# Copies and band writes issued by SyncE, and a new order of units and weights in the last part

## The chip, the core and the metric

The kernel runs on one core of a Trainium2 chip. A core has five engines that work side by side and meet at semaphores: TensorE (PE, matmuls; its weight loads are listed as PEld), VectorE (DVE), ScalarE (ACT), GpSimd (POOL) and SyncE (SP, which here only issues DMAs). Each engine executes its instructions in the order of the program. All DMAs, whoever issues them, are moved by the core's sixteen DMA engines. The metric is device time in microseconds; lower is better.

## The reference

All data is float32. The input x has the shape (2, 256, 64, 64). Two layers follow each other:

```python
# layer 0: full attention over the 4096 positions of an image, 8 heads of 32
q, k, v = conv1x1(x, Wq, bq) / sqrt(32), conv1x1(x, Wk, bk), conv1x1(x, Wv, bv)
fuse = softmax(q @ k.T) @ v
x = conv1x1(concat([x, fuse]), Wf, bf) * m + x * (1 - m)     # m: mask, resized bilinearly
# layer 1
x = x * sigmoid(relu(xp @ ca_w1 + ca_b1) @ ca_w2 + ca_b2)    # per position
x = x + window_attention(x)                                  # 8 x 8 windows, 4 heads of 64
x = channel_shuffle(x, groups=4)
y = relu(bn1(grouped_conv7x7(x, sa_w1)))                     # 64 groups: 4 channels in, 1 out
y = bn2(grouped_conv7x7(y, sa_w2))                           # 64 groups: 1 channel in, 4 out
return x * sigmoid(y)
```

What matters for the change is the pair of 7 x 7 convolutions at the end, and the attention loop ahead of it, since the preparation of the convolutions' weights runs beside that loop.

## The kernel before

**Three parts.** First come the projections: q, k and v of all sixteen chunks (two images of eight chunks, a chunk being 512 positions) are computed and written to DRAM. Then the attention loop runs over 1024 slots: for each image b, chunk c, half of the heads g and block m of 128 keys, PE computes four score matmuls (L632), ACT the exponentials (L642), PE the products with the values (L661), and DVE adds up the denominators (L663). Work on a finished chunk (fusion L731, layer 1's gate, the window attention up to L963) is cut into small stages which `run_stages` sets between the slots of the next chunk. The result of a chunk goes as rows to the DRAM tensor `x_s` (L978, `xs` in the profile). The last part is the pair of convolutions, as a generator `convolve` whose steps lie between the stages of the last chunk, and run alone after them.

**Order.** The program's order is written out by hand (`manual_schedule`): every engine executes what is emitted for it, in that order. SyncE's list in the loop is made of the key and value pieces (`load_piece`, L559 and L561, one piece for four slots, two pieces ahead, three buffers each), q, x and the mask of the next chunk. A load waits on SyncE until PE has left the buffer that it fills.

**Bands.** The convolutions are matmuls with banded weights. A unit is four groups of channels; there are NU = 16 units. The weights of unit u are one row block of the DRAM tensor `w_s` (`ws` in the profile): 128 x 1792 floats, 896 KB, of which most are zero. The generator `bands` fills it: sixteen copies of a block of zeros (L341), then 156 small DMAs from DRAM to DRAM which write the coefficients onto diagonals (L349, L355 and L362), in runs of 28 floats for the first convolution and of 7 floats for the second. `bands` is advanced by one DMA at every fifth slot (L1189). GpSimd issues all of them. Its other work in the loop is the storing of rows (L978). What is left of `bands` would be emitted at slot 960, before the generator `convolve` starts (L1171).

**Convolution items.** The list `items` (L987) holds pairs of a unit and the images that it is done for: units 0 to 6 for image 0 alone, which is complete before the last chunk is; units 2 to 6 for image 1; units 7 to 15 for both; and units 1 and 0 for image 1. `EARLY = 7` sets the border. For each item k the generator emits `conv1(k + 1)` (L1043 and L1051), `conv2(k)` (L1067, L1077, L1083) and `gate(k)` (L1089 and the stores of L1102). So on PE the first convolution of item k + 1 stands ahead of the second one of item k.

**Inputs of the items.** `load_x` (L1022) reads the rows: image 0's early items into four tiles `xe`, later ones into four tiles `xl`, which come free with the end of the loop. `more` issues the first four of these as soon as the last stage has been emitted, so on SyncE they stand there and wait for the rows of image 1 to land in `x_s`. `load_w` (L1015) reads a unit's weights: unit 0 into a tile of its own, all others into a ring of EB = 8 buffers that held the exponentials. Before the change, units 1 to 8 are loaded one behind the other when the loop ends, and units 9 to 15 and once more unit 1 (the list `again`) after an item that used a weight for the last time. Stores of `gate` alternate between GpSimd and SyncE; for early items that are stored after the last stage GpSimd issues all.

Of the kernel before, what the change touches and what calls it, by code (L numbers as in the profile page):

```python
# [17 lines left out]
B, C, H, W = 2, 256, 64, 64  # L18
# [11 lines left out]
AHEAD = 2  # L30
EB = 8
DN = 8
EARLY = 7
HEADS1, HD1 = 4, 64
WS = 8
NW = W // WS
# [10 lines left out]
NU = NG // UG  # L47
# [8 lines left out]
def conv_seq_kernel(ctx: ExitStack, tc: tile.TileContext, a, out):  # L56
    nc = tc.nc
# [68 lines left out]
    w_s = dram.tile([NU, P, 2 * 32 * UW], F32, name="ws")  # L126
# [33 lines left out]
    zero_s = dram.tile([P, 2 * 32 * UW], F32, name="zeros")  # L160
# [171 lines left out]
    def spread(row, n):  # L332
        f = row.shape[-1]
        return row.rearrange("p u f -> u p f").to_broadcast([NU, n, f])


    def bands():
        band1 = w_s.rearrange("u p (m f) -> u (p m) f", f=UW)
        band2 = w_s.rearrange("u p (m f) -> u (p m) f", f=UW // 4)
        for u in range(NU):  # L340
            nc.gpsimd.dma_start(w_s[u], zero_s)  # L341
            yield
        for q in range(4):
            for dy in range(KS):
                r0, r1 = max(0, dy - PAD), min(RB, RB + dy - PAD)
                p0, m0, n = 32 * q + 1 + r0, 1 + r0 - dy + PAD, r1 - r0
                k = KS * q + dy
                at0, step = p0 * 64 + m0, 64 + 1
                nc.gpsimd.dma_start(  # L349
                    band1[:, at0 : at0 + step * (n - 1) + 1 : step, :], spread(r1_s[k : k + 1], n)  # L350
                )
                yield
                for i in range(4):
                    at0, step = p0 * 256 + 128 + i * 32 + m0, 256 + 1
                    nc.gpsimd.dma_start(  # L355
                        band2[:, at0 : at0 + step * (n - 1) + 1 : step, :],
                        spread(r2_s[k : k + 1, :, i], n),
                    )
                    yield
            for i in range(4):  # L360
                at0 = 32 * q * 256 + 128 + i * 32 + 1
                nc.gpsimd.dma_start(  # L362
                    band2[:, at0 : at0 + RB, :], spread(r2_s[32 + q : 33 + q, :, i], RB)
                )
                yield
# [157 lines left out]
    def pipeline(arm, shifted, pools):  # L523
# [462 lines left out]

        items = [(u, (0,)) for u in range(EARLY)] + [(u, (1,)) for u in range(2, EARLY)]  # L987
        items += [(u, (0, 1)) for u in range(EARLY, NU)] + [(1, (1,)), (0, (1,))]
        staged = []

        def convolve():
# [8 lines left out]
                nc.gpsimd.memset(t, 0.0)  # L1000
                ycs.append(t)
            xs, ws, ys = {}, {}, {}
            again = deque([*range(1 + EB, NU), 1])
            dst = out.rearrange("b (g i) r w -> b i r g w", i=4)

            def load_w(u):
                if u >= NU:
                    return
                n = 2 * 32 * UW
                if u == 0:  # L1010
                    t = cpool.tile([P, n], F32, name=f"w{arm}{u}")
                else:
                    t = ep.tile([P, HG, CH], F32, tag="e", name=f"w{arm}{u}")
                    t = t.rearrange("p h n -> p (h n)")[:, 0:n]
                nc.sync.dma_start(t, w_s[u])  # L1015
                ws[u] = t

            def load_x(k):
                u, images = items[k]
                x = xs[k] = early[k % 4] if k < EARLY else xcs[k % 4]  # L1020
                for i, b in enumerate(images):
# [5 lines left out]
            def load_rows(k):  # L1027

                while len(xs) < min(k + 1, len(items)) and (
                    staged or B - 1 not in items[len(xs)][1]  # L1030
                ):
                    load_x(len(xs))

            def conv1(k):
                if k >= len(items):
                    return
                u, images = items[k]
                n = nb * len(images)
                w = ws[u][:, 0 : 32 * UW].rearrange("p (m g d) -> p g d m", g=UG, d=KS)
                s = psum1(f"c1{arm}{k}")  # L1040
                for d in range(KS):
                    for j in range(4):
                        nc.tensor.matmul(  # L1043
                            s[32 * j : 32 * j + 32, 0 : n * W],
                            w[:, j, d, :],
                            xs[k][:, 0:n, j, d : d + W],
                            start=(d == 0),
                            stop=(d == KS - 1),
                        )
                y = ys[k] = ycs[k % 2]  # L1050
                nc.scalar.activation(  # L1051
                    y[:, 0:n, PAD : PAD + W],
                    s[:, 0 : n * W].rearrange("p (n x) -> p n x", x=W),
                    AF.Relu,
                    bias=cbias1[:, u : u + 1],
                )

            def conv2(k):
                u, images = items[k]
                n = nb * len(images)  # L1060
                y = ys.pop(k)
                w = ws[u][:, 32 * UW :].rearrange("p (m d) -> p d m", d=KS)
                tiles = [psum2(f"c2{arm}{k}_{hh}") for hh in range(2)]
                for d in range(KS):
                    for j in range(4):
                        r = slice(32 * j, 32 * j + 32)
                        nc.tensor.matmul(  # L1067
                            tiles[j // 2][:, j % 2, 0 : n * W],
                            w[r, d],
                            y[r, 0:n, d : d + W],  # L1070
                            start=(d == 0),
                            stop=(d == KS - 1),
                        )
                z = pool.tile([P, 4, B * nb * W], F32, tag="z", name=f"z{arm}{k}", bufs=2)
                z = z[:, :, 0 : n * W]
                for hh in range(2):
                    nc.scalar.activation(  # L1077
                        z[:, 2 * hh : 2 * hh + 2, :],
                        tiles[hh][:, :, 0 : n * W],
                        AF.Tanh,  # L1080
                        scale=0.5,
                    )
                nc.scalar.activation(z, z, AF.Copy, bias=0.25, scale=0.25)  # L1083
                return z.rearrange("p j (n x) -> p j n x", x=W)

            def gate(k, z):
# [5 lines left out]
                if k == len(items) - 1:  # L1092
                    engines = (nc.scalar, nc.sync)
                elif staged and k < EARLY:
                    engines = (nc.gpsimd,)
# [12 lines left out]
            def more():  # L1108
                if staged and not xcs:

                    for n in range(3):
                        t = ep.tile([P, HG, CH], F32, tag="sum", name=f"xl{arm}{n}", bufs=3)
                        t = t.rearrange("p h n -> p (h n)")[:, 0 : B * nb * UG * WP]
                        xcs.append(t.rearrange("p (n g w) -> p n g w", n=B * nb, g=UG, w=WP))
                    xcs.append(pool.tile([P, B * nb, UG, WP], F32, name=f"xl{arm}3"))
                    load_rows(EARLY + 3)
                return bool(xcs)
# [2 lines left out]
            load_rows(3)  # L1120
            load_w(0)
            pool = yield
            for u in range(1, 1 + EB):
                load_w(u)
            conv1(0)
            yield
            for k, (u, images) in enumerate(items):
                while len(xs) <= k + 1 < len(items):
                    if not more():
                        yield  # L1130
                conv1(k + 1)
                yield
                more()
                z = conv2(k)
                yield
                more()
                gate(k, z)
                if xcs or k + 4 < EARLY:
                    load_rows(k + 4)

                if (u >= 2) == (B - 1 in images) and u and again:
                    load_w(again.popleft())

        def run_later():
            for _ in range(len(later)):
# [6 lines left out]
        def run_stages():  # L1152
            while stages:
# [3 lines left out]
                stages.popleft()  # L1157

        banded = bands()

        nc.scalar.activation(warm, ones[0:1, 0:1], AF.Exp)
# [132 lines left out]
```

## Time and profile before

| what | value |
|---|---|
| median of three runs | 3051.75 us (3051.0 to 3055.79) |
| the profiled execution | 3062.01 us, of it 3060.2 from first to last instruction |
| PE busy | 2967.3 us (97%) |
| DVE busy | 2498.5 us (82%) |
| ACT busy | 2478.7 us (81%) |
| POOL busy | 369.4 us (12%) |
| zero copies L341 | 16 of 896 KB, issued 188.8 to 216.1 us |
| band DMAs L349, L355, L362 | 156, issued 241.2 to 2346.2 us |
| weight loads L1015 | 17 of 896 KB, 2659.8 to 2980.1 us |
| attention loop | starts at 187.1 us |
| last part | about 2814 us to the end |

Busy time says how much of the span an engine had an instruction in work; the sum over parts with different limits hides where time is lost. Times in the views count from the first instruction. In a timeline, a line is start, length, engine, line of the code, operation, written tile, read tile, number of instructions, and in brackets how long the engine idled before and who released it. `SPq` stands for DMAs issued on SyncE's queue; `issue` stands for time in which the profile shows nothing that the engine waited for. Buffer numbers are left out of names, and an added `a` is the name of the arm of the program that is run (`ka` is a key piece).

### The profile page before, as it was taken

The page shows a single profiled execution, that of the slowest core. Times are in us where ns is not written, and L with a number is a line of the kernel's source. Part 1 is how long each engine was busy: PE and PEld are TensorE (multiplying, and loading weights), DVE is VectorE, ACT ScalarE, POOL GpSimd, SP SyncE. Part 2 cuts the span into 40 slices and gives each one's busy share as a digit, 9 for nine tenths or more (in the row PEclk, how much of TensorE's full clock was granted, in tenths as well). Part 3 has the DMA queues.
Part 4 walks back from the last instruction along what each step waited for, and adds up shares of the span by engine and source line. Part 5 has one row for each costly group of instructions (what it writes and reads, how often), then busy time and mean ns, then how long its engine had stood idle before and what let it go on. Part 6 is the DMA issues. An engine that isn't in the chain of part 4 may idle for free.

```text
span 3060.2 us, 60785 instructions
## 1 busy us (share of the span) xinstructions
PE 2967.3 (97%) x25114; PEld 1005.6 (33%) x25114; DVE 2498.5 (82%) x1347; ACT 2478.7 (81%) x4147; POOL 369.4 (12%) x636
## 2 busy tenths in 40 slices
PE   9968989999999999999999999999999999999897
PEld 3541222222322222232222232322222322223675
DVE  3227989899989999899999898999999898999211
ACT  5537969898989899898989898989898898988333
POOL 8020000101010101010100101010101000000256
PEclk9988999999999999999999999999999999999999
DMA  8574212424252424243322314242424232423364
GB/s 241 200 248 106 63 52 60 71 63 73 60 78 60 70 70 73 67 66 75 63 65 64 68 60 73 62 71 60 69 71 71 66 71 66 102 63 101 96 208 112
DMA packets 155999, 266.02 MB, mean 87 GB/s; under 512 B 43016, under 2 KB 61756, under 8 KB 155456
## 3 DMA queue, kind: packets, MB, share of 16 engines
q1 hardware_dynamic: 127424, 213.86, 25.3%
q0 software_dynamic: 23728, 45.48, 9.8%
q8 instruction: 200, 3.28, 0.5%
q10 hardware_dynamic: 4560, 2.70, 0.3%
q14 instruction: 87, 0.71, 0.1%
HBM read 213.49 MB, written 66.13 MB: 91 GB/s over the span
## 4 chain that ended last, share of the span: by engine, by line
PE 71%; DVE 13%; DMA 4%; issue 2%; ACT 2%; POOL 1%; SPq 0%; DVEq 0%; ACTq 0%
PE sa L632 29%; PE ava L661 27%; DVE suma L663 11%; PE qka L802 4%; PE hya L731 4%; DMA ka<-ks 2%; PE vwa L888 2%; ACT ea L642 1%; PE opa L952 1%; PE c2a L1067 1%; POOL out_dram L1102 1%; DMA wa<-ws 1%; PE c1a L1043 1%; PE sca L836 1%; PE rda L699 1%
## 5 line engine op out<-in xcount | busy, mean ns | idle before, releaser
L663 DVE TENSOR_TENSOR suma<-suma,ea 128x2048 f32<-128x2048 f32 x960 | 2198.7, 2290 | 122.7 <-ACT ea L642 39.5
L642 ACT ACTIVATE ea<-sa 128x512 f32<-128x512 f32 (+1 forms) x3072 | 2043.7, 745 | 122.0 <-PE sa L632 75.4
L632 PE MATMUL sa<-qa,ka 32*128 32x512 f32 x8192 | 1186.6, 641 | 39.7 <-DMA ka<-ks 38.2
L661 PE MATMUL ava<-ea,va 128*32 128x512 f32 x8192 | 1093.8, 605 | 0.3 <-ACT fa L671 0.3
L632 PEld LDWEIGHTS sa<-qa,ka 32*128 32x128 f32 x8192 | 331.2, 183 | 793.6 <-ACT ea L642 688.7
L661 PEld LDWEIGHTS ava<-ea,va 128*32 128x32 f32 x8192 | 161.8, 108 | 781.9 <-issue 755.7
L978 POOL DMA_DIRECT2D xs<-xo x94 | 66.1, 711 | 2302.4 <-DVE xo L963 2302.2
L1102 POOL DMA_DIRECT2D out_dram<-za x204 | 114.9, 571 | 102.4 <-DVE za L1089 55.5
L802 PE MATMUL qka<-ua,qkv_w 128*128 128x512 f32 x256 | 118.4, 605 | 0.0
L663 DVE TENSOR_TENSOR suma<-ea,ea 128x2048 f32<-128x2048 f32 x32 | 73.1, 2285 | 51.3 <-ACT ea L642 51.3
L1089 DVE TENSOR_TENSOR za<-za,xla 128x1536 f32<-128x1536 f32 (+1 forms) x16 | 22.6, 1409 | 110.0 <-ACT za L1083 56.7
L453 DVE TENSOR_REDUCE top<-sq 128x512 f32<-128x2048 f32 x16 | 36.6, 2286 | 81.4 <-ACT sq L447 81.4
L739 ACT ACTIVATE ta<-hya,bf 128x512 f32<-128x512 f32 x32 | 20.3, 684 | 99.7 <-PE hya L731 99.7
L1067 PE MATMUL c2a<-yca,wa 32*128 32x192 f32 (+1 forms) x1288 | 95.9, 440 | 4.0 <-issue 3.8
L1077 ACT ACTIVATE za<-c2a 128x384 f32<-128x384 f32 (+1 forms) x46 | 25.8, 615 | 86.3 <-DMA out_dram<-za 50.2
L743 DVE TENSOR_TENSOR ta<-ta,mca 128x512 f32<-128x512 f32 x32 | 22.0, 689 | 88.3 <-ACT ta L739 88.3
L1067 PEld LDWEIGHTS c2a<-yca,wa 32*128 32x128 f32 x1288 | 87.0, 314 | 14.9 <-issue 14.0
L857 ACT ACTIVATE ewa<-ewa,mxwa 128x64 f32<-128x64 f32 x256 | 85.5, 362 | 1.5 <-DVE mxwa L848 1.5
L355 POOL DMA_DIRECT2D ws<-r2s x112 | 69.7, 625 | 95.3 <-DMA ws<-r2s 48.6
L815 ACT ACTIVATE qka<-qka,qkv_b 128x512 f32<-128x512 f32 x64 | 40.7, 695 | 41.6 <-PE qka L802 41.6
L802 PEld LDWEIGHTS qka<-ua,qkv_w 128*128 128x128 f32 x256 | 46.0, 189 | 71.3 <-issue 58.7
L434 PE MATMUL q<-x,WqT 128*128 128x512 f32 x128 | 62.2, 631 | 5.6 <-DMA WqT<-in_WqT_dram 5.6
(141 smaller groups left out, 1620.5 us busy)
## 6 DMA issues: line engine op xcount, KB each, us to landing
ka<-ks SPq DMA_DIRECT2D x256, 256.0 KB
va<-vs SPq DMA_DIRECT2D x256, 256.0 KB
wa<-ws SPq DMA_DIRECT2D x17, 896.0 KB
ws<-zeros POOLq DMA_DIRECT2D x16, 896.0 KB, 23.9
xs<-xo POOLq DMA_DIRECT2D x78, 140.0 KB, 8.0
xla<-xs SPq DMA_DIRECT2D x25, 420.0 KB
x<-in_x_dram SPq DMA_DIRECT2D x16, 512.0 KB
qs<-qst SPq DMA_DIRECT2D x16, 512.0 KB
```

Of the source, the lines that this page charges most:

```text
L355: nc.gpsimd.dma_start(band2[:, at0 : at0 + step * (n - 1) + 1 : step, :], spread(r2_s[k : k + 1, :, i], n),)
L434: nc.tensor.matmul(s[:, g, :], w[:, kc, g * P : (g + 1) * P], rhs, start=(kc == 0), stop=(kc == KC - 1),)
L632: nc.tensor.matmul(heads[j], k[r, cols], q[r, g, :], start=True, stop=not shifted)
L642: nc.scalar.activation(e[:, h, :], tile, AF.Exp, scale=SCALE0)
L661: nc.tensor.matmul(av[r, :], v[:, m % PB, r], e[:, j, :], start=start, stop=stop)
L663: nc.vector.tensor_add(total, first[0] if m == 1 else total, e)
L731: nc.tensor.matmul(s[:, oc, :], wf[:, kc, oc * P : (oc + 1) * P], f[:, kc - KC, :] if half else xw[kc], start=(kc == 0), stop=(kc == 2 * K ...
L802: nc.tensor.matmul(s[:, j, :], wqkv[:, kc, o : o + P], u[:, kc, :], start=(kc == 0), stop=(kc == KC - 1),)
L857: nc.scalar.activation(e[:, n, :], e[:, n, :], AF.Exp, bias=mx[:, n : n + 1], accum_out=rs[:, n : n + 1],)
L978: eng.dma_start(x_s[b, n, p + r0 : p + r1].rearrange("r g w -> g r w"), xo[64 * h : 64 * h + 64, oc, r0 - WS * c : r1 - WS * c, :],)
L1067: nc.tensor.matmul(tiles[j // 2][:, j % 2, 0 : n * W], w[r, d], y[r, 0:n, d : d + W], start=(d == 0), stop=(d == KS - 1),)
L1102: engines[stores % len(engines)].dma_start(dst[b, i, r0:r1, UG * u : UG * u + UG, :], z[p + r0 : p + r1, :, nb * m + n, :],)
```

## The change

All DMAs of `bands`, the sixteen zero copies and the 156 band writes, are issued by SyncE in the place where GpSimd issued them. `EARLY` becomes 8: unit 7 is done for image 0 among the early items and for image 1 after them, and no longer for both at once. So there are 24 items and not 23. Of the weights, only units 1 and 2 are loaded when the loop ends; after the gate of each item one further unit is loaded, in the order 3 to 15 and then 1 again. After item 7 none is loaded.

```diff
-EARLY = 7
+EARLY = 8
@@ bands()
-            nc.gpsimd.dma_start(w_s[u], zero_s)
+            nc.sync.dma_start(w_s[u], zero_s)
...
-                nc.gpsimd.dma_start(
+                nc.sync.dma_start(
                     band1[:, at0 : at0 + step * (n - 1) + 1 : step, :], spread(r1_s[k : k + 1], n)
                 )
...
-                    nc.gpsimd.dma_start(
+                    nc.sync.dma_start(
                         band2[:, at0 : at0 + step * (n - 1) + 1 : step, :],
                         spread(r2_s[k : k + 1, :, i], n),
                     )
...
-                nc.gpsimd.dma_start(
+                nc.sync.dma_start(
                     band2[:, at0 : at0 + RB, :], spread(r2_s[32 + q : 33 + q, :, i], RB)
                 )
@@ convolve()
-            again = deque([*range(1 + EB, NU), 1])
+
+            weights = deque([*range(1, NU), 1])
...
-            for u in range(1, 1 + EB):
-                load_w(u)
+            for _ in range(2):
+                load_w(weights.popleft())
             conv1(0)
...
-                if (u >= 2) == (B - 1 in images) and u and again:
-                    load_w(again.popleft())
+                if weights and (k < EARLY - 1 or k >= EARLY):
+                    load_w(weights.popleft())
```

## The prediction

> **What bounds the kernel now.** I read the list of engines first (PE busy 97%, DVE 82%), then the waits, then PE's timeline round every wait over 1 us, then windows there. In the attention loop PE gives no time away: a chunk of 64 slots takes 163.2 us (the fusion matmuls of L731 start at 2206.14, 2369.32 and 2532.50 in the chain). So only two places can give time back, the start of the loop and the last part. PE's timeline at the start:
>
> ```profile
> 202.32 1.06 PE L661 MATMUL ava<-ea,va 128*32 128x512 f32 x8
> 241.08 2.09 PE L632 MATMUL sa<-qa,ka 32*128 32x512 f32 x8 [37.69 <-DMA ka<-ks]
> ```
>
> PE waits 37.69 us for the third key piece. SyncE issued that load at 192.12. Stretches of the same time (us, then busy time of PE, PEld, DVE, ACT, POOL, then clock, DMA share, GB/s), and the DMA view for the second stretch:
>
> ```profile
> 187.00:203.00 16.00, 15.61 (x112) 4.19 (x112) 10.13 (x5) 15.71 (x26) 6.47 (x13) 1.00 0.97 326
> 203.00:241.00 38.00, 0.39 (x4) 0.00 (x0) 5.91 (x3) 1.41 (x3) 2.44 (x5) 0.54 0.96 311
> ```
> ```profile
> q0 software_dynamic: 371, 10.21, 80.0%
> q1 hardware_dynamic: 863, 1.59, 15.6%
> ```
>
> All engines idle while the DMA engines run full: POOL's queue q0 holds 80% with the sixteen zero copies, SyncE's queue q1 gets 15.6% (packets, MB, share). Key pieces arrive when the zeros are through. DVE's timeline carries the loss on:
>
> ```profile
> 194.85 14.27 DVE L663 TENSOR_TENSOR suma<-suma,ea 128x2048 f32<-128x2048 f32 x6
> 245.19 2.29 DVE L663 TENSOR_TENSOR suma<-suma,ea 128x2048 f32<-128x2048 f32 x1 [36.07 <-ACT ea L642]
> 249.10 52.61 DVE L663 TENSOR_TENSOR suma<-suma,ea 128x2048 f32<-128x2048 f32 x22 [1.62 <-ACT ea L642]
> ```
>
> From 249.10 DVE runs without a gap until the first stage, and at 398.49 PE itself has waited 8.99 us and starts only when DVE's reciprocal (397.45) is there. So in the first chunk DVE sets the pace (2.39 us a slot against PE's 2.07), and what it lost, 36.07 + 1.62 = 37.69 us, is on the path. After 398 PE sets the pace.
>
> The last part, PE's timeline:
>
> ```profile
> 2833.75 2.65 PE L1067 MATMUL c2a<-yca,wa 32*128 32x192 f32 x40
> 2840.19 1.68 PE L1067 MATMUL c2a<-yca,wa 32*128 32x192 f32 x16 [3.79 <-issue]
> 2843.60 6.02 PE L731 MATMUL hya<-xa,WfT 128*128 128x512 f32 x8
> 2849.45 3.60 PE L731 MATMUL hya<-fa,WfT 128*128 128x512 f32 x8
> 2900.84 3.56 PE L1067 MATMUL c2a<-yca,wa 32*128 32x192 f32 x56
> 2908.44 4.72 PE L1043 MATMUL c1a<-xla,wa 128*32 128x192 f32 x56 [4.04 <-DMA xla<-xs]
> ```
>
> Two gaps: 3.79 us in the middle of a group of 56, with nothing waited for, and 4.04 us for the rows of image 1. The first lies inside the burst of eight weight loads. Stretches, and SyncE's queue:
>
> ```profile
> 2814.00:2842.00 28.00, 23.62 (x333) 13.75 (x334) 18.23 (x11) 12.92 (x22) 2.77 (x4) 0.93 0.93 283
> 2842.00:2853.00 11.00, 11.00 (x35) 5.25 (x31) 1.23 (x1) 2.58 (x5) 0.00 (x0) 0.71 0.01 5
> ```
> ```profile
> 2814.21 18.07 SPq L1015 DMA_DIRECT2D wa<-ws x8
> 2860.12 0.80 SPq L1022 DMA_DIRECT2D xea<-xs x1
> 2896.42 1.37 SPq L978 DMA_DIRECT2D xs<-xo x2
> 2904.72 1.99 SPq L1022 DMA_DIRECT2D xla<-xs x4
> ```
>
> The clock after the gap is 0.5 until about 2848.8: the same eight L731 matmuls take 6.02 us, then 3.60. From 2908.44 to 3043 PE has no gap over 0.2 us.
>
> **What the Trainium skill says.** "DMA: Bandwidth & Descriptors", section "Queues, rings and completion order": an engine takes turns between the queues at packet granularity. The trace agrees: in the stall q0's packets average 27.5 KB (10.21/371), q1's 1.8 KB (1.59/863), and q1 moves 1.59 MB in 38 us. The same page, "Issuing engines are not separate DMA queues": another issuer saves only issue time. That would leave the copies as heavy as before; here I count on their place in the order of issue, not on the issuer. "TensorE: Matmul & The Clock Gate", Part 1: after an idle window of about 3.4 us the clock halves. The trace agrees: 0.5 after 3.79 and after 4.04 us.
>
> **Part 1, zeros on SyncE.** POOL issues all sixteen at 188.84 to 216.09, held back by nothing but their own completions. SyncE executes in order between the key and value loads, which wait for PE (L559 and L561 waits). So it issues one per five slots: 5 x 2.07 = 10.3 us apart at least. One copy costs about 52/16 = 3.3 us of all DMA engines (188.8 to 241 for sixteen, other loads included). Piece 2 comes ahead of the first zero copy: 192.12 issue, 1.28 MB (x, mask, k, v) at 390 GB/s (loads reach 399 in the window at 2870) is 3.3 us, so by about 197, before the need at 203.4. Later pieces have 17.4 us between issue and first use (251.45 to slot 20, which is ten slots after the one at 248.13: 268.8) and are held 3.3 us at most. Gain 37.69. Bounds: 25 if later pieces stumble, 40 if more than DVE's own idle returns.
>
> **Part 2, bands on SyncE.** 156 DMAs (28 of L349, 112 of L355, 16 of L362); with the zeros 172 issues, which one per five slots ends at slot 860, before the flush at slot 960. POOL pays 0.62 us each; SyncE's small issues take 0.32 to 0.8 us, and it has waits of 4 to 5 us per load in which that disappears. Data: from 542 to 556 thirteen bands and two pieces keep the DMA share at 5.80 x 2 us = 11.6 us, so about 1 us a band. The trace shows no such band on q1. Lower bound 0.5; upper 14, the landing time with several in flight (medians of 9.3 to 13.9 for the forms of L355 and L362). I take 1 to 3 us. A piece has 17.4 us of cover, so nothing reaches PE: cost 0. POOL has nothing late behind it. No band waits long on SyncE: the first needs the sixteenth zero copy, issued about 10 us before; behind such a wait stand the key loads, again with 17.4 us.
>
> **Part 3, weights one at a time.** Only w1 and w2 are loaded at 2814. The burst (896 KB x 8) is gone, so I count the fetch gap and its slow clock away: L731's second half starts at 2842.1 instead of 2849.45 (c2 ends 2837.3, spreads 2838.4, 3.63 us for the first half; the other inputs, via ACT and DVE, are there by 2841). Gain 7.35; bounds 0 (the gap comes from something else) and 8.
>
> Against it, each weight now follows the gate three items earlier. A load issued at 2868.36 is in by about 2873.1 (windows: 399 and 220 GB/s, then 0), so 5 us. Relative to before: w3 goes out at 2861.0, in at 2866.5, wanted at 2866.09: 0.4. w5 out 2884.1, in 2889.5, wanted 2888.77: 0.7. w4 has 7 us to spare; w6 comes with what is lost already. Together 1.2.
>
> **Part 4, eight units early.** Unit 7 is done twice alone (2 x 5.98: 2.46 + 3.52) instead of once for both images (9.64): +2.32 us of PE. The extra early item should fill the 4.04 us gap, but its weights can't be there: w7 is issued after gate 4, and the four loads of image 1 rows stand ahead of it on SyncE, blocked until the stores have landed (2904.72, now 2906.5 with the 1.2 and w6 beside the stores). They took 7.1 us of traffic (to 2911.8), w7 another 2.4: in at 2916.5. On PE the first convolution of item 7 stands ahead of the second of item 6, so PE idles from 2905.6 to 2916.5. It resumes 2916.5 - 7.35 = 2909.15 against 2908.44: +0.7. Slow clock as before, +0.2.
>
> **Sum.** -37.7 (start) + 0.7 + 0.2 + 2.3 (last part, in which the 7.35 is used up) = -34.5. The profiled execution, 3062.01 (span 3060.2, 1.8 around it), becomes 3027.5. It lay 10.3 above the median of the runs, so I take the difference to the median: 3051.75 - 34.5 = 3017.
>
> **Rivals.**
> 1. Forecast, 3017, own range 3008 to 3027: chance 0.54.
> 2. The stall only shrinks: zero copies on the loads' own queue hold pieces 3 to 10 up. For: every load from 193 on now stands behind one. Against: 3.3 us against 17.4. About 17 us stay: 3034. 0.14 (0.01 of it within 0.2%).
> 3. The last part is better: w7 in time, 4.04 filled, no idle of 10.9: 3017 - 10 = 3007. The order on SyncE speaks against. 0.10.
> 4. The last part is worse: the gap in the group stays (+7.35) or weights come later: 3026. 0.09.
> 5. Slower: bands as small packets on q1 saturate the loads' queue. Five slots last 12.75 us (163.2/64 x 5) and carry 640 KB of loads, 1.65 us at 390 GB/s, so bands decide from about 11 us each; from 11.2 the 34.5 are lost (156 x 0.22), at 12, inside the upper bound, they cost 156 us: 3173. For: never seen on q1, runs of 28 bytes. Against: 1 us on q0. 0.13.
>
> **Numbers.** Three runs spread 3051.0 to 3055.79, so 0.2% (6 us) is what can be told. Faster 0.86, within 0.01, slower 0.13. Range 3004 to 3040: cases 1 to 4; case 5 stays out.
>
> **What would show it.** Right: no PE wait on ka<-ks over 1 us near 203, L341 on SPq about 10 us apart, the first c2a group whole near 2796 with clock 1.0, one PE gap of some 10 us ahead of a c1a, released by wa<-ws, then 24 items. Wrong: PE waits on ka or va spread over the loop every five slots (case 5), or a wait of tens of us near 200 (case 2); no gap at c1a (case 3).

## The result and the profile after

The changed kernel takes 3025.45 us (median of four runs, 3024.80 to 3025.97), the kernel before 3053.71 us in the same comparison (3051.00 to 3055.79). The ratio is 0.9908, with a 95% interval from 0.9891 to 0.9925: faster by 28.3 us. The forecast was 3017 us, 34.5 us faster. The profiled execution of the changed kernel took 3024.80 us (span 3023.0), 0.65 us below the median; that of the kernel before, 3062.01, had lain 8.3 us above the median.

Line numbers are one to two higher than before (L632 is L633, L1067 is L1069). In the names of tiles, `c1a` and `c2a` are the results of the first and second convolution, `hya` that of the fusion, `ca1a` that of layer 1's gate; items are counted from 0. First PE's timeline, the two longest waits between the start of the loop and the last part (the next ones are 1.10 us at 1668.48 and 1.09 us at 2647.93); a row is start, length, engine, line, operation, written and read tile, number of instructions, and the wait ahead of it:

```profile
187.35 3.06 PE L633 MATMUL sa<-qa,ka 32*128 32x512 f32 x16 [1.19 <-ACT vst L480]
361.21 1.01 PE L700 MATMUL rda<-inva,spread_h 32*128 32x128 f32 x6 [8.99 <-issue]
```

The 37.69 us wait for the third key piece is gone. The wait at the first stage, 8.99 us, is the same as before and 37.28 us earlier (398.49 to 361.21): PE still waits there for DVE. DVE's timeline shows why the whole gain came through, a run of additions without the hole of 36 us:

```profile
195.06 69.38 DVE L664 TENSOR_TENSOR suma<-suma,ea 128x2048 f32<-128x2048 f32 x29
```

SyncE's queue at the start shows the copies between the loads, and the same stretch of time as before shows what that does to all engines (us, busy time of PE, PEld, DVE, ACT, POOL, then clock, DMA share, GB/s):

```profile
193.25 0.42 SPq L562 DMA_DIRECT2D va<-vs  x1
193.73 0.59 SPq L342 DMA_DIRECT2D ws<-zeros  x1
194.45 0.48 SPq L560 DMA_DIRECT2D ka<-ks  x1
199.53 0.32 SPq L562 DMA_DIRECT2D va<-vs  x1
199.90 0.48 SPq L342 DMA_DIRECT2D ws<-zeros  x1
```
```profile
203.00:241.00 38.00, 38.00 (x300) 8.73 (x296) 36.34 (x17) 36.82 (x56) 0.00 (x0) 1.00 0.43 146
```

PE was busy for 0.39 us of these 38 and is now for all of them. The DMA engines are busy for 43% and not for 96%: the same sixteen copies are spread out to 368 us.

The last part on PE:

```profile
2792.98 3.58 PE L1069 MATMUL c2a<-yca,wa 32*128 32x192 f32 x56
...
2797.78 3.70 PE L732 MATMUL hya<-xa,WfT 128*128 128x512 f32 x8
2801.32 3.60 PE L732 MATMUL hya<-fa,WfT 128*128 128x512 f32 x8
...
2818.67 2.54 PE L1045 MATMUL c1a<-xea,wa 128*32 128x192 f32 x56 [0.65 <-DMA wa<-ws]
...
2843.36 2.55 PE L1045 MATMUL c1a<-xea,wa 128*32 128x192 f32 x56 [1.92 <-DMA wa<-ws]
...
2853.35 2.54 PE L1045 MATMUL c1a<-xea,wa 128*32 128x192 f32 x56 [0.32 <-DMA wa<-ws]
...
2868.72 4.72 PE L1045 MATMUL c1a<-xea,wa 128*32 128x192 f32 x56 [9.33 <-DMA wa<-ws]
```

The first c2a group is whole, with no gap and no half clock after it. In its place stand four waits for weights, together 12.22 us, the longest at the eighth early item. SyncE's queue there has the order that the forecast named, the three weight loads behind the four loads of rows:

```profile
2858.37 1.99 SPq L1024 DMA_DIRECT2D xla<-xs x4
2860.40 1.51 SPq L1017 DMA_DIRECT2D wa<-ws x3
```

(Both rows are from the timeline of the queue; the kernel stores nothing through SyncE in between.) At the end there is a wait that was not foreseen: PE waits for ACT, and ACT for a buffer of results (`z`) whose stores are not out yet. Here is the last group of matmuls, first before and then after the change:

```profile
3039.84 3.56 PE L1067 MATMUL c2a<-yca,wa 32*128 32x192 f32 x52 [0.17 <-ACT za L1077]
```
```profile
3005.51 4.51 PE L1069 MATMUL c2a<-yca,wa 32*128 32x192 f32 x52 [2.54 <-ACT za L1079]
```

This wait costs nothing in the end: the last matmul ends at 3010.02, and ACT takes its result up only at 3013.10, when stores of `za` have landed once more. From the start of the `c2a` row ahead of this group (3035.65 before, 2998.94 after) to the end of the span it is 24.55 us before and 24.06 us after.

Put together along PE, from profile to profile:

| stretch, by its ends on PE | before | after | difference |
|---|---|---|---|
| start to the first stage (L699 / L700 at 398.49 / 361.21) | 398.49 | 361.21 | -37.3 |
| from there to the second c1a of the last part | 2431.05 | 2427.56 | -3.5 |
| from there to the second part of ca1a (2856.66 / 2808.53) | 27.12 | 19.76 | -7.4 |
| from there to the c1a of item 7 (2908.44 / 2868.72) | 51.78 | 60.19 | +8.4 |
| from there to the end of the last c2a | 134.96 | 141.30 | +6.3 |
| from there to the end of the span | 16.80 | 12.98 | -3.8 |
| span | 3060.2 | 3023.0 | -37.2 |

The last four rows before the sum are the last part: -7.4 + 8.4 + 6.3 - 3.8 = +3.5 us.

### The profile page after: what moved, and what is told of

It reads as the page before. It is cut to its first block, busy times and chain, and to the rows that moved or that the text cites. A ratio compares the mean times of both kernels' runs of the same rounds, so it can differ in the third digit from the quotient of the medians.

```text
span 3023.0 us, 61011 instructions
## 1 busy us (share of the span) xinstructions
PE 2962.5 (98%) x25226; PEld 1009.9 (33%) x25226; DVE 2498.7 (83%) x1348; ACT 2479.5 (82%) x4151; POOL 267.0 (9%) x470
## 4 chain that ended last, share of the span: by engine, by line
PE 72%; DVE 18%; issue 3%; ACT 2%; DMA 2%; POOL 2%; SPq 0%; DVEq 0%; ACTq 0%; POOLq 0%
PE sa L633 27%; PE ava L662 25%; DVE suma L664 16%; PE hya L732 4%; PE qka L803 4%; PE vwa L889 2%; PE v L472 2%; PE q L435 2%; PE k L435 2%; POOL out_dram L1104 2%; ACT ea L643 1%; DMA out_dram<-za 1%; PE c1a L1045 1%; PE sca L837 1%; DVE za L1091 1%
## 5 line engine op out<-in xcount | busy, mean ns | idle before, releaser
L633 PE MATMUL sa<-qa,ka 32*128 32x512 f32 x8192 | 1187.1, 640 | 1.5 <-ACT vst L480 1.2
L633 PEld LDWEIGHTS sa<-qa,ka 32*128 32x128 f32 x8192 | 332.7, 183 | 754.6 <-ACT ea L643 687.8
L1091 DVE TENSOR_TENSOR za<-za,xla 128x768 f32<-128x768 f32 (+1 forms) x16 | 21.8, 1359 | 108.4 <-ACT za L1085 68.4
L1069 PE MATMUL c2a<-yca,wa 32*128 32x192 f32 (+1 forms) x1344 | 98.2, 436 | 2.5 <-ACT za L1079 2.5
L1069 PEld LDWEIGHTS c2a<-yca,wa 32*128 32x128 f32 x1344 | 89.7, 315 | 13.2 <-issue 9.9
L889 PE MATMUL vwa<-qkv_w,ua 128*128 128x256 f32 x256 | 59.5, 386 | 0.0
```

The source lines that it names most:

```text
L633: nc.tensor.matmul(heads[j], k[r, cols], q[r, g, :], start=True, stop=not shifted)
L889: nc.tensor.matmul(sv[:, t, :], u[:, kc, t * P : (t + 1) * P], wqkv[:, kc, 2 * C : 3 * C], start=(kc == 0), stop=(kc == KC - 1),)
L1069: nc.tensor.matmul(tiles[j // 2][:, j % 2, 0 : n * W], w[r, d], y[r, 0:n, d : d + W], start=(d == 0), stop=(d == KS - 1),)
```

## The experiments

Medians and ratios are against the kernel before, run on the same chip in between. Where an experiment has no interval, it is a single execution with its profile.

**The kernel before once more.** No edit.

> The kernel before, unchanged, profiled once more. The profile of before lay 8.3 us above its median (3062.0 against 3053.7), the profile of after lay on its median. Theory A (the gap of 3.79 us in the c2a group and its slow clock, 7.4 us together, happen in some executions only): the profiled time is near 3054, the wait on ka<-ks is again 37 to 38 us, and the c2a group of the first item is whole. Theory B (the stall at the start varies): the wait on ka<-ks is some 30 us and the gap in the c2a group is there again. Theory C (profiling alone costs before 8 us): 3062 again, with both.

It took 3055.49 us. PE's timeline:

```profile
240.79 2.09 PE L632 MATMUL sa<-qa,ka 32*128 32x512 f32 x8 [37.35 <-DMA ka<-ks]
```
```profile
2835.70 1.68 PE L1067 MATMUL c2a<-yca,wa 32*128 32x192 f32 x16 [1.82 <-issue]
2839.11 5.24 PE L731 MATMUL hya<-xa,WfT 128*128 128x512 f32 x8
2844.18 3.60 PE L731 MATMUL hya<-fa,WfT 128*128 128x512 f32 x8
```

None of the three theories is right as it was put. The wait at the start is as long as before (37.35 us). The gap in the c2a group is there, so it is not rare, but it varies: 1.82 us here and 3.79 us in the first profile. From the start of c2a to the second half of L731 it is 12.95 us here and 15.70 there, against 8.34 in the changed kernel: the gap and the half clock cost 4.6 us in this execution and 7.4 in that one. The rest of the 6.5 us between the two spans is spread in pieces of 0.6 to 1.3 us over the other stretches.

**Only the copies and bands on SyncE** (the last part as before):

```diff
-            nc.gpsimd.dma_start(w_s[u], zero_s)
+            nc.sync.dma_start(w_s[u], zero_s)
...
-                nc.gpsimd.dma_start(      # and the three band writes alike
+                nc.sync.dma_start(
```

> Zeros and bands issued by SyncE, the last part as before. If the forecast's sum holds part by part: -37.7 by the start, 3.2 us better than after in the profile since the last part costs +3.2 there, so by profile the same gap of 3.79 us in the c2a group. Theory A (that gap is rare): 3053.7 - 40 = about 3014, clearly below after (3025.5). Theory B (the stall at the start is smaller in most executions): about 3053.7 - 30 = 3024.

3020.06 us, ratio 0.9883 (0.9868 to 0.9898), so 35.4 us faster, and faster than the whole change. No wait on a key or value piece over 0.45 us. The gap in the c2a group is there, and so is the burst of eight weight loads:

```profile
2800.45 1.26 PE L1067 MATMUL c2a<-yca,wa 32*128 32x192 f32 x16 [3.22 <-issue]
```

The time lies between what theories A and B said. What it settles is the share: the copies and bands bring all of the gain, and the new last part gives some 5 us of it back.

**Only the new last part** (bands on GpSimd as before):

```diff
-EARLY = 7
+EARLY = 8
...
-            for u in range(1, 1 + EB):
-                load_w(u)
+            for _ in range(2):
+                load_w(weights.popleft())
...
```

> Only the last part changed (eight early units, weights one at a time), zeros and bands on GpSimd as before. Theory A (gap rare): the last part costs what the w7 wait and the extra item cost, +10 to +12 us: about 3064. Theory B (gap there in most executions): +3 us: about 3057. In the profile: ka<-ks wait of 37.7 us, waits on wa<-ws of 0.7, 1.9, 0.3 and 9.3 us as in after.

3065.45 us, ratio 1.0033 (1.0020 to 1.0045): slower by 10 us. The start's wait is 37.23 us. PE waits for weights ahead of the same groups as in the changed kernel, 1.36, 2.12 and 8.91 us (only the wait of 0.3 us is gone), the longest in PE's timeline:

```profile
2911.74 4.72 PE L1045 MATMUL c1a<-xea,wa 128*32 128x192 f32 x56 [8.91 <-DMA wa<-ws]
```

This is theory A's number, though for another reason: the gap is not rare before, but it costs less in the other profiles than the 7.4 us of the first. Against the second profile of the kernel before, the last part of this run takes 9.2 us longer. The profiled execution (3069.36 us, the longest of six) also has a wait of 3.54 us in the loop (at 1378.93), put down to nothing; after the first stage no other profile has one of over 1.21 us in the loop. How much of it is in the median of the six runs is not known.

**Only the zero copies on SyncE**, bands on GpSimd, last part as before; the edit is the first pair of lines of the diff for copies and bands.

> Only the sixteen zero copies issued by SyncE; bands on GpSimd and the last part as before. Theory: the zero copies alone make the start stall; same as the run with zeros and bands on SyncE within 4 us, no wait on ka<-ks over 1 us. Rival: the bands' bursts on GpSimd also cost; then 3 us or more slower than that run, with PE waits after the row stores of a chunk.

3019.23 us, ratio 0.9877 (0.9861 to 0.9892). With and without the bands the time is the same within the noise (0.8 us between medians whose runs spread over 3.8 and 6.8 us), and there is no wait on a key piece over 0.45 us. So the sixteen copies were the whole of the stall, and where the 156 band writes are issued shows no effect on the time.

**Four weights first.** The changed kernel, with each weight issued two items earlier and none before its buffer is free:

```diff
-            for _ in range(2):
+            for _ in range(4):
                 load_w(weights.popleft())
...
-                if weights and (k < EARLY - 1 or k >= EARLY):
+                if weights and (weights[0] <= EB + 1 or k >= EARLY):
```

> The changed kernel, but with four weights loaded when the loop ends and not two, so that each later weight is issued two items earlier and w7 goes out after gate 2, ahead of the four loads of image 1 rows. Theory (the order on SyncE makes w7 late): the waits of 0.7, 1.9, 0.3 and 9.3 us on wa<-ws are gone, no other PE wait over 3 us takes their place, 12 us faster than after: about 3013. Rival (DMA is the limit there, the order only decides who waits): PE waits for xla or wa by 5 us or more, about 3020.

3013.88 us, ratio 0.9870 (0.9853 to 0.9886), 11.6 us below the changed kernel, by medians of two comparisons. All four waits for weights are gone, no gap in the c2a group came back, and the rows of image 1 are in time. What is left on PE are waits for result buffers:

```profile
2885.57 4.25 PE L1069 MATMUL c2a<-yca,wa 32*128 32x192 f32 x52 [1.34 <-ACT za L1079]
...
2994.30 4.87 PE L1069 MATMUL c2a<-yca,wa 32*128 32x192 f32 x52 [2.54 <-ACT za L1079]
```

So the order on SyncE, not the DMA engines' rate, had made the weights late.

**The same with seven early units:**

```diff
-EARLY = 8
+EARLY = 7
```

> As the run with four weights ahead, but with seven early units as before. Theory (the extra early item fills the wait for the rows of image 1 of 3.3 to 4 us and costs 2.3 us of PE): 1 to 2 us slower than eight units, with a PE wait on xla<-xs of 3 to 4 us and half a clock after it. Rival (the eighth early unit is worth nothing or less): same or faster.

3011.48 us (3010.08 to 3012.28; with eight units 3013.37 to 3014.34 in the same comparison), ratio 0.9862 (0.9845 to 0.9878). This is the fastest version. It has the wait that the eighth unit should have filled, in PE's timeline:

```profile
2859.87 2.55 PE L1045 MATMUL c1a<-xla,wa 128*32 128x192 f32 x56 [2.73 <-DMA xla<-xs]
```

It is 2.73 us and the next groups run at full clock. The expectation was the wrong way round: the eighth early unit costs 2.4 us. In the profiles, from the second `c1a` of the last part to the end, it is 4.0 us: 2.3 us of added matmuls and 4.3 us at the two groups with waits for result buffers in the middle of the last part (0.29 and 1.34 us, with the slow matmuls after the second), less 2.8 us at the rows of image 1, and 0.2 us for all that comes from the last `c2a` on. The last wait of 2.54 us therefore costs next to nothing: with seven units, where that wait is 0.76 us, the work after the last matmul takes 2.9 us longer.

**All copies on SyncE in one burst:**

```diff
         for u in range(NU):
             nc.sync.dma_start(w_s[u], zero_s)
-            yield
+        yield
```

> Zeros and bands on SyncE, last part as before, but all sixteen zero copies issued together on SyncE at the second slot. Theory (the pace made by the place between the loads takes the stall away, not the issuer): key piece 3, issued behind the copies, lands some 50 us later, PE waits 25 to 40 us at about 212 to 215, 3045 to 3060. Rival (the issuer matters, GpSimd's copies being the heavy ones): no wait over 5 us, about 3020.

3046.23 us. SyncE's queue, and PE's timeline:

```profile
193.62 27.62 SPq L341 DMA_DIRECT2D ws<-zeros  x16
223.60 0.33 SPq L559 DMA_DIRECT2D ka<-ks  x1
```
```profile
243.85 2.09 PE L632 MATMUL sa<-qa,ka 32*128 32x512 f32 x8 [31.94 <-DMA ka<-ks]
```

The stall is back with SyncE as the issuer. It comes one piece later, since piece 2 was ahead of the copies; piece 3 first waits for the issue of the copies, until 223.60, and then for their data. So it is the pace, one copy between two loads, that removed it.

**The burst on GpSimd, later:**

```diff
-            if i % 5 == 1:
+            if i % 4 == 1 and i > 140:
                 next(banded, None)
```

> The kernel before, with bands emitted from slot 141 on (one per four slots), so that on GpSimd the zero copies stand behind the row stores of the first chunk and go out in a burst near 540 us minus the start stall. Theory (a burst on GpSimd starves the loads wherever it is): no wait near 203, and a PE wait of 25 to 40 us on ka<-ks near 520 to 560; about 3050. Rival (only the start is vulnerable, since there no pieces are ahead): wait under 10 us, about 3022.

3028.34 us. GpSimd's list now has the row stores of the first chunk ahead of the copies. Twelve of them, and not sixteen as the expectation had it, go out from 501.8 us, the other four behind the next chunk's stores. PE's timeline:

```profile
524.68 1.14 PE L661 MATMUL ava<-ea,va 128*32 128x512 f32 x8 [2.19 <-DMA va<-vs]
...
536.62 2.09 PE L632 MATMUL sa<-qa,ka 32*128 32x512 f32 x8 [6.59 <-DMA ka<-ks]
```

The waits sum to 8.8 us, and the time is 9.1 us above that of the run with only the zero copies on SyncE. This is the rival's size of wait (under 10 us) and far from the theory's 25 to 40 us. The burst does starve the loads in the middle of the loop too, but there it costs a quarter of what it costs at the start. Twelve copies are three quarters of the sixteen, and PE ran on for 20.7 us after the first copy before it waited, against 14.6 us at the start. That these two make the whole difference is not shown.

**Eight copies in a burst on GpSimd, then eight on ScalarE** (the other eight on SyncE, one per five slots; last part as before):

```diff
+            if u < 8:
+                nc.gpsimd.dma_start(w_s[u], zero_s)      # nc.scalar in the other run
+                if u < 7:
+                    continue
+            else:
+                nc.sync.dma_start(w_s[u], zero_s)
```

> Bands on SyncE, last part as before; of the zero copies the first eight are issued by GpSimd at once, the other eight by SyncE one per five slots. Theory (queues take turns by packets, and GpSimd's are the large ones): key piece 2 gets through only when the eight copies are nearly done, 26 us after 189; PE wait on ka<-ks of 8 to 14 us. Rival (bytes decide, whatever the queue): the same wait as with the eight on ScalarE.

> As the run with eight zero copies on GpSimd, but these eight are issued by ScalarE, a hardware queue of its own. Theory (packets): rows of 7 KB as packets against the loads' 2 KB, so the loads keep a fifth to a quarter of the traffic and piece 2 lands near 203 to 208: PE wait on ka<-ks under 5 us; ScalarE itself is held some 4 us by the issues. Rival (bytes decide): 8 to 14 us as on GpSimd.

On GpSimd 3034.23 us, and on PE

```profile
219.31 2.09 PE L637 MATMUL sa<-qa,ka 32*128 32x512 f32 x8 [15.44 <-DMA ka<-ks]
```

Half of the burst costs somewhat under half of the wait, and more than the 8 to 14 us that the theory had. On ScalarE 3024.61 us and no wait on a key piece over 0.45 us; PE waited 2.42 and 0.67 us for exponentials. But that comparison is not clean: by the timelines, ScalarE issued its copies from 195.11 on, behind the issue of piece 2 (193.50), while GpSimd had begun at 189.32.

**Eight copies on ScalarE ahead of its first exponential:**

```diff
         banded = bands()
+        next(banded)
```

> In the run with eight copies on ScalarE they went out at 195 to 201, behind the issue of key piece 2 (193.5), so it said little. Here ScalarE issues them before its first exponentials, about 188 to 192, ahead of piece 2 as GpSimd did. Theory (packets): the loads keep a share by packets of 7 KB against 2 KB, piece 2 lands well before the copies are through; wait on ka<-ks under 8 us, against 15.4 with GpSimd. Rival (bytes, or copies of any queue that come first go first): 12 us or more.

3043.45 us. ScalarE's timeline, with the queue's line from the DMA view of 187 to 220 us (packets, MB, share):

```profile
186.60 24.65 ACTq L342 DMA_DIRECT2D ws<-zeros  x8
211.28 1.28 ACT L1167 ACT_TABLE_LOAD   x1 [24.47 <-issue]
```
```profile
q10 hardware_dynamic: 256, 7.34, 62.6%
```

The issues themselves held ScalarE for 24.65 us, not for the 4 us expected when they were issued later, and PE waited 24.41 us for the exponentials. So the run says nothing of how long piece 2 was held up. Nor are the packets of this queue 7 KB: 7.34 MB in 256 packets are 28.7 KB each, as large as GpSimd's. Whether the loads' small share in a burst is due to the sizes of packets stays open.

## Why the prediction came out as it did

The time lay inside the range and the direction was right. Part by part, with the first profile of the kernel before, from which the forecast was made:

- **The stall at the start (-37.69).** Right in its mechanism and nearly in size. By profile, the first stage comes 37.28 us earlier; by times, the copies alone bring 36.2 us and copies with bands 35.4. The run with the burst on SyncE shows that the place in the order did it and not the issuer: in the burst (one execution) about 7 us of the gain were left. This agrees with the sentence of the Trainium skill that the text on record names (DMA: Bandwidth & Descriptors, "Issuing engines are not separate DMA queues"). The copies went out closer together than forecast, at first 6 to 8 us apart (193.73, 199.90, 208.22) and not 10.3, the last at 368.4; still no later piece stumbled (rival 2).
- **The loop after the start (0).** The forecast had nothing here. It was 3.5 us shorter after the change, and 2.2 us against the second profile of the kernel before. This stretch, from the first stage to the second `c1a` of the last part, takes 2428.8 to 2434.5 us in the four profiles with the bands on GpSimd (the run with the late burst left out) and 2427.5 to 2429.0 us in the eight with the bands on SyncE. So the bands may have a part of a microsecond or two in it; the medians with and without them do not show it.
- **Bands on SyncE (0).** Right by times: with bands on GpSimd the time is the same within the noise. Rival 5, the saturated queue, had 0.13 and did not come. Over the whole span the bands take even less of the DMA engines on SyncE's queue. Between the run with only the zero copies on SyncE and the one with copies and bands there, the share of q1 and q0 together falls from 26.2% + 7.9% to 27.0% + 4.2%, although packets under 512 B rise from 43016 to 114056.
- **The gap in the c2a group (-7.35).** The gap left, and by profile L731's second half gained 7.36 us on the groups ahead of it. But 7.35 was the value of one execution, and the largest of all. In the nine profiles with the burst of eight weights the gap is there with 1.56 to 3.79 us, and the gap and its slow clock cost 4.6 to 7.4 us, on average 5.9; in the four without the burst there is none. The run with four weights first and seven early units differs from the one with only copies and bands on SyncE in the order of the weights alone, and the gap is gone. So that the burst makes the gap is shown; that it is instruction fetch standing behind the burst is only argued.
- **Weights one at a time (0.4 + 0.7, together 1.2 up to item 6).** 0.65 + 1.92 + 0.32 = 2.89 us: the right places, and too small by 1.7. Most of it is the wait of 1.92 us for w5, which ends 6.6 us after its load was issued (2836.73); the forecast had 5.4 us. Why that load took longer is not shown.
- **Item 7's weights (idle of 10.9, +0.7 net).** Right in its mechanism: 9.33 us at the c1a of item 7, behind the loads of rows. 11.6 us came back when all weights were issued two items earlier, w7 ahead of the rows. The two errors in the weights, +1.7 and -1.6, cancel: up to item 7 the last part stands at -7.4 + 8.4 = +1.0 us, against +0.7.
- **The extra item (+2.3 + 0.2).** Right in sum, though not in its parts. From item 7 to the last c2a the changed kernel takes 6.3 us more, but 3.8 us of that come back after the last matmul, so +2.5 us remain. The 2.54 us wait for a result buffer and the half clock after it, which no step of the forecast had, lie ahead of stores that set the end (the last `c2a` is taken up by ACT 3.1 us after it is done).
- **From the profile to the median.** This is the step that fitted least. The sum was right for the execution that it was made from: -34.5 forecast, -37.2 found, and 3027.5 forecast for a profiled execution that took 3024.8. Then the difference was set against the median of the runs, as if the 10.3 us by which that execution lay above it would stay. They did not: the profiled execution of the changed kernel lies at its median, 8 us above the forecast of 3017. The second profile of the kernel before, 3055.49, has all the same waits, with a smaller gap. Against that one the start gives -36.0 us, the loop -2.2, and the last part costs +7.5 instead of +3.5, since less is saved by the gap. By times it is 3025.45 against 3020.06 of the run with copies and bands alone, +5.4, and +10 in the run with the last part alone. The number of rival 4, 3026, came out, but not for its reason, since the gap left.

Two sums of the forecast do not come out as they are written, and neither decides anything. The weights of item 7 would be in at 2906.5 + 7.1 + 2.4 = 2916.0, not 2916.5. In rival 5 the bands would decide from 12.75 - 1.65 = 11.1 us each, so the 34.5 us would be lost at 11.3 and not at 11.2, and 12 us each would give about 3157 and not 3173.

## What to carry to other kernels

In this kernel the background copies belong between the loads of an engine that the consumer paces. An engine with nothing to wait for sent them all at once, and the whole core stalled beside full DMA engines. Before a load is delayed to smooth a burst, list what stands ahead of its new place in the queue: here four loads blocked by stores made one set of weights 9 us late, and loading all sets two items earlier gave 11.6 us back. Price a loss of a few microseconds with its spread over executions: one gap cost between 4.6 and 7.4 us here, and the forecast had taken the upper end. And follow a wait to the end of the span before it is counted: the last wait of 2.54 us here moved nothing.

## What was unexpected in the hardware

A burst of large copies from DRAM to DRAM goes out fast only at its beginning. Of sixteen copies of 896 KB, GpSimd issued eight within 4.1 us (188.84 to 192.96) and the other eight one by one until 216.6, each after an earlier one had landed. SyncE took 6.0 us for its first eight and 27.62 us for all sixteen, against 27.7 us on GpSimd. On ScalarE the same eight copies took 5.7 us in one run (from 195.11) and 24.65 us in the other (from 186.60), where PE lost 24.41 us to it; what makes that difference is not shown.

Small band writes (runs of 28 to 112 bytes, 12 to 52 KB in each DMA) cost SyncE 0.54 us of issue each (median; up to 1.58) and no more DMA time than from GpSimd, where the forecast had found no row to price them from.

A short gap can be followed by a slow TensorE. The Trainium skill (TensorE: Matmul & The Clock Gate, Part 1) speaks of an idle window of about 3.4 us. In the second profile of the kernel before, a gap of 1.82 us was followed by half clock. Its windows (columns as in the first table of windows; the clock is the third number from the end):

```profile
2836.00:2838.00 2.00, 2.00 (x26) 1.96 (x25) 0.00 (x0) 0.59 (x2) 0.00 (x0) 0.50 0.86 352
```

In the changed kernel the clock was still 1.00 in the wait of 2.54 us near the end (3003 to 3005) and 0.50 only after PE had resumed (3007 to 3009). After the 2.73 us wait of the run with seven early units the next groups were at full clock (1.00 from 2859 to 2867). So here the length of the idle time alone does not tell when the clock drops.
